# A state-space scan emitted beside local attention and feed-forward, with its input replicated over states by DMA

## The chip, the cores and the metric

The kernel runs on one core of one Trainium2 chip. The metric is device time in microseconds (us) of one execution; lower is better. The core's engines are PE (TensorE: matmuls and transposes; PEld is its weight load), DVE (VectorE), ACT (ScalarE), POOL (GpSimd) and SP (SyncE), which here only issues DMAs. Each engine works through its own queue of instructions in order and waits on semaphores for the others. Everything is in fp32.

## What is computed

The input x has 32 sequences of 256 tokens of width 256. The output is x plus a two-layer attention and feed-forward network applied to the result of a state-space block:

```python
# state-space block (d_inner 512, 16 states)
xr, gate = split(x @ W_in.T); xr = xr + t_emb
xc = silu(causal_conv4(xr) + b_conv)
xn = layernorm(xc) * ln_g + ln_b
Bm, Cm, dt = split(xn @ W_xproj.T)            # 16 columns each
dt = tanh(dt @ W_dt.T + b_dt) * 0.01
Ad = 1 + dt * (-tanh(A_log)); Bd = Bm * min(norm(xn), 1)
h  = clip(h * Ad_t + Bd_t * xn_t, -10, 10)    # 256 steps, h is 16 x 512
y_t = sum over states of C_t * h
out = ((y + D * xn) * silu(gate)) @ W_out.T
# then twice: x += local_attention(shift(x)); x += geglu(layernorm(shift(x)))
```

The attention has 8 heads of 64 and windows of 128 tokens, each of which sees itself and the window before; q and k are normalized and rotated. The feed-forward has 682 hidden columns and uses gelu.

## The kernel before, in words

**Groups and stages.** The 32 sequences are worked on in four groups of eight (`GB`). One group's scan (`group_scan`, line 195) writes the group's residual `res`, and then two layers of `attention` (L472) and `feed_forward` (L617) update it in place; we call these two the blocks. The main loop (L712 to L720) emits scan, layer 0, layer 1 for group 0, then the same for group 1, and so on. `res` has one buffer, and scan, attention and feed-forward each open tile pools of their own and close them, so that each stage may use all of SBUF and all eight PSUM banks. All layer weights are loaded once at the start.

**The scan.** First the projection, the 4-tap convolution and silu are done for the whole group (L206 to L240: PE L210, ACT L221, POOL L226, DVE L231, ACT L236). Then there are 16 blocks of 16 steps. `prep` makes for a block of 128 (step, sequence) tokens the normalized `xn` (transposed on PE, L264; statistics L270), transposes it again (L293) to project B, C and dt (L301), and brings these through narrow products (L309 to L355) into the layout in which the scan needs them: 8 sequences x 16 states on the 128 partitions, steps in the free dimension. The kernel scales the state by the running product of Ad, so that a step is a clipped addition whose limits `lim` are scaled too. For each step, PE makes `bx` in PSUM (L413), which replicates a token's xn over its sequence's 16 states and multiplies by B: the stationary operand `lb` holds a diagonal of B values, 32 rows by 128 columns. DVE then computes one step (L421), `h_new = clip(h_old + bx)`, with one custom instruction of 128x512. For every four steps, PE sums over states with the C values (L429): the stationary operand is 128 x 32, and each of the four steps fills its own 32 rows of the PSUM tile `y`. At the end of a block, `z = (xn*D + y) * silu(gate)` is made (L439 to L441), transposed (L444) and, every four blocks, projected into `res` (L458, L465). The gate is a product of each block (L376).

**The blocks.** For a sequence, attention makes v, q and k of both windows (L497), squares and sums q and k (L508, L510), takes the inverse root with a POOL power (L192), rotates (L518 to L527) and transposes (L530). Then come, four or two heads at a time, the scores (L553), mask and maximum (L561, L565), exponential with sum (L569), transposition (L578), copy (L580) and the product with v (L583); every second sequence the output projection (L607) is added to `res` (L615). Feed-forward takes two sequences at once: layer normalization with transpositions (L641 to L660), two products per chunk of 128 hidden columns (L674), gelu (L682), product (L685), and after all six chunks the second projection (L692). In layer 1 it loads x (L634), adds it on POOL (L709) and stores the result (L710).

**What sets the order.** The kernel is written in a framework that finds the dependences, places the semaphores, and orders the instructions of each engine when the program is built; what is emitted earlier goes first where several instructions could go. So the order on an engine isn't that of the text: in the trace the preparation of the next scan block stands among the steps of the current one. A tile waits until a buffer of its pool and tag is free. All DMAs of the main part are issued by SP, in one order.

Of the kernel before, what the change touches and what calls it, by code (L numbers as in the profile page):

```python
# [9 lines left out]
FP = mybir.dt.float32  # L10
# [3 lines left out]
PSUM = bass.MemoryType.PSUM  # L14

# [7 lines left out]
GB = 8  # L23
TB = P // GB
NTB = S // TB
NQ = 4
NI = TB // NQ
TAPS = 4
# [11 lines left out]
def bc(ap, axis, n):  # L40

    ap = ap.unsqueeze(axis)
    shape = list(ap.shape)
    shape[axis] = n
    return ap.broadcast_to(shape)


@with_exitstack
def kernel(
# [35 lines left out]
    xpool = ctx.enter_context(tc.tile_pool(name="xg", bufs=1))  # L85
    rpool = ctx.enter_context(tc.tile_pool(name="res", bufs=1))

    def load_x(g):
        t = xpool.tile([P, KM, GB, S], FP, tag="xg", name=f"xg_{g}")
        for k in range(KM):  # L90
            nc.sync.dma_start(out=t[:, k], in_=xT[:, k, g * GB : (g + 1) * GB, :])
        return t
# [5 lines left out]

    w_in_sb = loaded(w_inT, [P, KM, 2 * DI], "w_in_sb", nc.sync)
# [3 lines left out]
    xg = load_x(0)  # L103
# [3 lines left out]
    wx_sb = loaded(w_xT, [P, NC_, 3 * NS], "wx_sb")  # L107
    wdt_sb = loaded(w_dtT, [NS, NS], "wdt_sb")
    bdt_sb = loaded(b_dt.partition_broadcast(P), [P, NS], "bdt_sb")
    a_sb = loaded(a_log.partition_broadcast(P), [P, NS], "a_sb")  # L110
    w_out_sb = loaded(w_outT, [P, NC_, DM], "w_out_sb")
    wqkv_sb = loaded(wqkv, [P, L, KM, 3 * DI], "wqkv_sb", nc.sync)
    wo_sb = loaded(wo, [P, L, NC_, DM], "wo_sb", nc.sync)
    flg_sb = loaded(f_ln_g, [P, L, KM], "flg_sb")
    flb_sb = loaded(f_ln_b, [P, L, KM], "flb_sb")
    w1_sb = loaded(w1, [P, L, KM, 2 * HID], "w1_sb", nc.sync)
    b1_sb = loaded(b1, [P, L, 2, len(MCH)], "b1_sb")
    w2_sb = loaded(w2, [P, L, len(MCH), DM], "w2_sb", nc.sync)
    b2_sb = loaded(b2, [P, L, KM], "b2_sb")

# [3 lines left out]
    def sums(name, n, src, out=None):  # L124
        t = const.tile([P, n], FP, tag=name, name=name)
        nc.vector.tensor_reduce(t if out is None else out(t), src, AX.X, ALU.add)
        return t

    tok_seq = sums("tok_seq", GB, ident.rearrange("p (r b) -> p b r", b=GB))
    tok_step = sums(  # L130
        "tok_step", TB, ident.rearrange("p (q i b) -> p q i b", q=NQ, i=NI),
        lambda t: t.rearrange("p (i q) -> p q i", i=NI),
    )
    tok_row = sums("tok_row", 32, ident.rearrange("p (q r) -> p r q", q=NQ))
    st_seq = sums("st_seq", GB, ident.rearrange("p (b n) -> p b n", b=GB))
    st_n = sums("st_n", NS, ident.rearrange("p (b n) -> p n b", b=GB))
    zero_tb = const.tile([P, TB], FP, tag="zero_tb", name="zero_tb")
    nc.gpsimd.memset(zero_tb, 0.0)

    neg_half = const.tile([P, HEADS], FP, tag="neg_half", name="neg_half")  # L140
    nc.gpsimd.memset(neg_half, -0.5)
    half = const.tile([P, 1], FP, tag="half", name="half")
# [3 lines left out]
    a_row = const.tile([P, NS], FP, tag="a_row", name="a_row")  # L146
    nc.scalar.activation(a_row, a_sb, AF.Tanh)
    nc.vector.tensor_scalar(a_row, a_row, -1.0, 0.01, ALU.mult, ALU.mult)
# [13 lines left out]

    rc_sb = const.tile([P, L, NW, 2, DH], FP, tag="rc_sb", name="rc_sb")
    rs_sb = const.tile([P, L, NW, 2, DH], FP, tag="rs_sb", name="rs_sb")
    with tc.tile_pool(name="setup", bufs=2) as setup:
# [14 lines left out]


# [7 lines left out]
    def rsqrt(pool, src, n, name):  # L189

        r = pool.tile([P, n], FP, tag=f"{name}_r", name=f"{name}_r")
        nc.gpsimd.tensor_tensor(r, src, neg_half[:, 0:n], ALU.pow)  # L192
        return r

    def group_scan(g, xg, res):


        with ExitStack() as es:
            xcp = es.enter_context(tc.tile_pool(name=f"xc{g}", bufs=1, reuse_waits="tile"))

            xc = xcp.tile([P, NC_, NTB, NQ, NI, GB], FP, tag="xc", name=f"xc_{g}")

            with tc.tile_pool(name=f"cv{g}", bufs=2, reuse_waits="tile") as cv, tc.tile_pool(
                name=f"cvp{g}", bufs=4, space=PSUM, reuse_waits="tile"
            ) as cvp:
                for j in range(GB // 2):  # L206
                    for c in range(NC_):
                        ps = cvp.tile([P, 2, S], FP, tag="ps", name="ps")
                        for k in range(KM):
                            nc.tensor.matmul(  # L210
                                ps.rearrange("p b t -> p (b t)"),
                                w_in_sb[:, k, c * P : (c + 1) * P],
                                xg[:, k, 2 * j : 2 * j + 2, :].rearrange("p b t -> p (b t)"),
                                start=(k == 0),
                                stop=(k == KM - 1),
                            )
                        xr = cv.tile([P, 2, TAPS - 1 + S], FP, tag="xr", name="xr")
                        nc.gpsimd.memset(xr[:, :, 0 : TAPS - 1], 0.0)
                        for i in range(2):
                            b = g * GB + 2 * j + i  # L220
                            nc.scalar.activation(  # L221
                                xr[:, i, TAPS - 1 :], ps[:, i, :], AF.Identity,
                                bias=cond_sb[:, c, b : b + 1],
                            )
                        acc = cv.tile([P, 2, S], FP, tag="acc", name="acc")
                        nc.gpsimd.tensor_scalar(  # L226
                            acc, xr[:, :, 0:S], wc_sb[:, c, 0:1], bconv_sb[:, c : c + 1],
                            ALU.mult, ALU.add,
                        )
                        for k in range(1, TAPS):  # L230
                            nc.vector.scalar_tensor_tensor(  # L231
                                acc, xr[:, :, k : k + S], wc_sb[:, c, k : k + 1], acc,
                                ALU.mult, ALU.add,
                            )
                        for i in range(2):
                            nc.scalar.activation(  # L236
                                xc[:, c, :, :, :, 2 * j + i].rearrange("p n q i -> p n i q"),
                                acc[:, i].rearrange("p (n i q) -> p n i q", n=NTB, q=NQ),
                                AF.Silu,
                            )  # L240

            sp = es.enter_context(tc.tile_pool(name=f"sp{g}", bufs=2, reuse_waits="tile"))
            hp = es.enter_context(tc.tile_pool(name=f"hp{g}", bufs=8, reuse_waits="tile"))
            zp = es.enter_context(tc.tile_pool(name=f"zp{g}", bufs=1, reuse_waits="tile"))
            sm = es.enter_context(tc.tile_pool(name=f"sm{g}", bufs=2, reuse_waits="tile"))
            ps_bx = es.enter_context(
                tc.tile_pool(name=f"pbx{g}", bufs=1, space=PSUM, reuse_waits="tile")
# [152 lines left out]
            for tb in range(NTB):  # L400
                xn, lb, ct, lim, sg, p_end = nxt
                if tb + 1 < NTB:
                    nxt = prep(tb + 1, p_end)
# [425 lines left out]
```

## Time and profile before

| | us |
|---|---|
| median of 3 runs (7242.7 to 7244.15) | 7243.88 |
| the profiled execution, its own time | 7238.73 |
| its span, first to last instruction | 7236.7 |
| PE busy | 6051.1 (84%) |
| DVE busy | 2972.4 (41%) |
| POOL busy | 1775.1 (25%) |
| ACT busy | 1582.7 (22%) |
| DVE idle in front of the scan step (L421) | 759.9 |
| mean clock granted to TensorE | 0.815 of full |
| bytes moved by DMA | 40.36 MB |

Busy time is the union of the intervals in which an engine executes something; of PE it is partly modelled, since matmuls are pipelined. A row of a group shows the line, the engine, the operation, the tiles as out<-in with their shapes, the count, then the busy time in us and the mean duration in ns, and behind the second bar the engine's idle time in front of these instructions and what ended it. A window's row shows busy times of all engines in a stretch of the span. A row of a load shows its size and the time from issue to landing.

### The profile page before, as it was taken

How to read it: one execution, taken by the hardware profiler on the slowest of the kernel's cores; microseconds unless marked ns; L12 is line 12 of the kernel's file. 1: busy time of each engine (PE TensorE's matmuls, PEld its weight loads, DVE VectorE, ACT ScalarE, POOL GpSimd, SP SyncE). 2: the span in 40 equal slices, each digit the busy share in tenths (PEclk: the TensorE clock that was granted, in tenths of full speed). 3: DMA queues.
4: the chain of work that ended last, by engine and by line, in shares of the span. 5: the costliest groups of instructions: out<-in, count | busy, mean ns of one | idle time of the engine just before them, and what ended most of it. 6: DMA issues, size and time to landing. Idle time of an engine off the chain costs nothing. (4 is left out here: it accounts for less than half of the span.)

```text
span 7236.7 us, 55107 instructions
## 1 busy us (share of the span) xinstructions
PE 6051.1 (84%) x19776; PEld 2809.3 (39%) x19776; DVE 2972.4 (41%) x5670; ACT 1582.7 (22%) x4134; POOL 1775.1 (25%) x1906
## 2 busy tenths in 40 slices
PE   6988888888788888888878888888887888888888
PEld 2222553553222355355322235435532223543553
DVE  4444442442444444244244444424424444442442
ACT  2001331331200133133120013313312001321331
POOL 2222320330222232033022222213302222321320
PEclk8778878888877887888888788798887778879878
DMA  2000000000000000000000000000000000000000
GB/s 76 0 1 12 1 0 0 1 6 15 3 0 0 12 0 1 0 1 6 15 3 1 0 12 1 1 0 1 6 16 2 0 0 0 1 0 0 1 6 18
DMA packets 14017, 40.36 MB, mean 6 GB/s; under 512 B 2352, under 2 KB 3376, under 8 KB 12080
## 3 DMA queue, kind: packets, MB, share of 16 engines
q1 hardware_dynamic: 10832, 34.78, 1.3%
q8 instruction: 158, 2.59, 0.1%
q10 hardware_dynamic: 2912, 2.05, 0.1%
q14 instruction: 115, 0.94, 0.0%
HBM read 28.43 MB, written 8.39 MB: 5 GB/s over the span
## 5 line engine op out<-in xcount | busy, mean ns | idle before, releaser
L421 DVE CUSTOM_DVE_ANT_0 h<-h,bx,lim 128x512 f32<-128x512 f32 x1024 | 825.4, 806 | 759.9 <-PE bx L413 705.3
L429 PE MATMUL y<-h,ly 128*32 128x512 f32 x2048 | 857.1, 766 | 10.6 <-DVE h L421 10.6
L192 POOL TENSOR_TENSOR ss_r<-ss,neg_half 128x8 f32<-128x8 f32 x256 | 421.4, 1646 | 1780.2 <-DVE ss L514 1771.4
L497 PE MATMUL ps_qkv<-wqkv_sb,res 128*128 128x512 f32 x1536 | 735.5, 601 | 0.0
L413 PE MATMUL bx<-xn,lb 32*128 32x512 f32 x2048 | 733.2, 782 | 0.0
L553 PE MATMUL sc<-kT,qT 64*128 64x128 f32 (+1 forms) x2048 | 576.8, 424 | 27.0 <-ACT kT L535 27.0
L583 PEld LDWEIGHTS ov<-v_sb,pT 128*128 128x128 f32 x3072 | 481.9, 241 | 110.3 <-issue 41.5
L583 PE MATMUL ov<-v_sb,pT 128*128 128x64 f32 x3072 | 506.7, 327 | 8.4 <-DVE pT L580 6.6
L561 DVE TENSOR_TENSOR p_sb<-sc,mask 128x512 f32<-128x512 f32 x384 | 257.4, 682 | 584.8 <-PE sc L553 434.0
L569 ACT ACTIVATE p_sb<-p_sb,nmax 128x128 f32<-128x128 f32 (+1 forms) x1024 | 453.4, 445 | 202.0 <-DVE nmax L565 196.6
L530 PE MATMUL tr_qk<-ident,rot 128*128 128x128 f32 x1024 | 181.2, 304 | 374.2 <-POOL rot L527 367.3
L674 PE MATMUL pg<-hT,w_sb 128*128 128x512 f32 (+1 forms) x768 | 420.9, 676 | 7.3 <-ACT hT L660 4.4
L192 POOL TENSOR_TENSOR ve_r<-ve,neg_half 128x1 f32<-128x1 f32 x192 | 106.9, 557 | 1184.7 <-DVE ve L649 1028.5
L685 DVE SCALAR_TENSOR_TENSOR ag<-pa,b_sb,gl 128x512 f32<-128x512 f32 x192 | 143.9, 749 | 574.4 <-PE pa L674 574.4
L553 PEld LDWEIGHTS sc<-kT,qT 64*128 64x128 f32 x2048 | 302.3, 217 | 190.5 <-ACT kT L535 90.2
L674 PE MATMUL pa<-hT,w_sb 128*128 128x512 f32 (+1 forms) x768 | 367.7, 601 | 0.0
L578 PE MATMUL tr_p<-ident,p_sb 128*128 128x128 f32 x1536 | 358.6, 348 | 4.4 <-ACT p_sb L569 4.4
L413 PEld LDWEIGHTS bx<-xn,lb 32*128 32x128 f32 x2048 | 188.3, 218 | 442.6 <-issue 439.0
L692 PE MATMUL po_f<-ag,w_sb 128*128 128x512 f32 (+1 forms) x768 | 356.9, 609 | 0.0
L450 ACT COPY zT<-tz 128x512 f32<-128x512 f32 x64 | 37.5, 586 | 1424.5 <-PE tz L444 1424.5
L497 PEld LDWEIGHTS ps_qkv<-wqkv_sb,res 128*128 128x128 f32 x1536 | 264.9, 191 | 211.4 <-issue 211.4
L526 POOL TENSOR_TENSOR rot<-rot,swp 128x512 f32<-128x512 f32 x256 | 324.7, 1268 | 69.7 <-DVE swp L523 69.7
(322 smaller groups left out, 7145.9 us busy)
## 6 DMA issues: line engine op xcount, KB each, us to landing
xg<-in_xT_dram SPq DMA_DIRECT2D x8, 1024.0 KB, 6.5
xs<-in_xT_dram SPq DMA_DIRECT2D x16, 512.0 KB, 4.1
out_dram<-fo SPq DMA_DIRECT2D x32, 256.0 KB, 2.0
wqkv_sb<-in_wqkv_dram SPq DMA_DIRECT2D x1, 3072.0 KB, 12.2
w_sb<-in_w_dram SPq DMA_DIRECT2D x1, 2728.0 KB, 12.6
w_sb<-in_w_dram SPq DMA_DIRECT2D x1, 1536.0 KB, 16.0
w_in_sb<-in_w_inT_dram SPq DMA_DIRECT2D x1, 1024.0 KB, 5.3
wo_sb<-in_wo_dram SPq DMA_DIRECT2D x1, 1024.0 KB, 4.9
```

Source lines behind the costliest of these rows:

```text
L192: nc.gpsimd.tensor_tensor(r, src, neg_half[:, 0:n], ALU.pow)
L413: nc.tensor.matmul(bx, lb[rows, i * GB : (i + 1) * GB, :].rearrange("p b n -> p (b n)"), xn[rows, :], start=True, stop=True,)
L421: nc.vector._custom_dve(TENSOR_ADD_SAT, out=h_new, in0=h_old, in1=bx, s0=lim[:, 0, t : t + 1], s1=lim[:, 1, t : t + 1],)
L429: nc.tensor.matmul(y[32 * q : 32 * q + 32, :], lyt[:, 32 * t : 32 * t + 32], hs[q], start=(i == 0), stop=(i == NI - 1),)
L497: nc.tensor.matmul(ps, res[:, k, b, t0 : t0 + W], wqkv_sb[:, l, k, a * DI : (a + 1) * DI], start=(k == 0), stop=(k == KM - 1),)
L526: nc.gpsimd.tensor_add(rot, rot, swp)
L553: nc.tensor.matmul(sc[:, i, :], qT[rows, h0 + i, w * W : (w + 1) * W], kT[rows, h0 + i, k0 : k0 + nk], start=True, stop=True,)
L569: nc.scalar.activation(p_sb[:, i, :], p_sb[:, i, :], AF.Exp, bias=nmax[:, h : h + 1], accum_out=rsum[:, h : h + 1],)
L578: nc.tensor.transpose(tr[:, i, ks], p_sb[:, i, ks], ident)
L583: nc.tensor.matmul(ov[:, h, :], pT[:, i, kb * W : (kb + 1) * W], v_sb[:, k0 // W + kb, h * DH : (h + 1) * DH], start=(kb == 0), stop=(kb = ...
L674: nc.tensor.matmul(ps[0:n, :], w1_sb[:, l, k, half_ * HID + o : half_ * HID + o + n], hT[:, k].rearrange("p b t -> p (b t)"), start=(k == ...
L692: nc.tensor.matmul(po.rearrange("p b t -> p (b t)"), w2_sb[0:n, l, m, d * P : (d + 1) * P], ag[0:n, m, :], start=(m == 0), stop=(m == len( ...
```

## The change

The whole device part is rewritten around one idea of order, in these parts.

1. **Two streams.** `group_scan`, `attention` and `feed_forward` become generators that yield after a piece of work. The first group's scan is emitted alone. Then `side_by_side` emits the blocks of group g and, in proportion (87 scan pieces to 248 block pieces), the scan of group g+1; the last group's blocks have nothing beside them. `res` has two buffers.
2. **Replication by DMA.** `xn` is written to a DRAM scratch tile `xnd` (three buffers). For every two steps one DMA of 512 KB on SP reads the eight sequences' rows 16 times, once for each state, into `xrep` (four buffers). ACT multiplies it in place by `beta`, a value per partition and step, and the DVE step takes both inputs from SBUF. `bx` and `lb` on PE and POOL are gone. D*xn is also loaded from the scratch (`xd`, four DMAs per 16 steps) and multiplied on POOL.
3. **Chunks of 32 steps.** The convolution, which was done for the whole group first, is done for each chunk, with a carry of three tokens; the gate too. A chunk's preparation is split into pieces, one after every four steps of the chunk before. xn isn't transposed a second time: the projection of B, C and dt runs on the unnormalized `xc` (64 output rows, 256 columns), and mean and inverse deviation are applied to the result; W_dt and ln_g are multiplied into the projection at the start. The result is spread to partitions by three small DMAs (`rw`). silu is computed as x*(1+tanh(x/2)), with ACT's tanh and a DVE product, and the halves go into w_out and the normalization.
4. **Memory.** All pools stay open. The blocks share five PSUM banks, the scan has three. `sq`, `swp`, `o_sb` and `hn` share one tag of two buffers, q, k and v are tiles of one window (two or three buffers), and other tags are shared too.
5. **Weights** of a layer are loaded anew in each of the eight layer passes, into single buffers.
6. **Smaller edits in the blocks.** The scores of window 1 are products of 128 instead of 256 columns; the output projection is done for each sequence (256 columns instead of 512); in feed-forward the second projection follows each hidden chunk into two banks that are held through the loop; x is added per half.

The core of the diff, shortened ("..." marks what is left out):

```diff
+CH = 32
+XR = 2
+def side_by_side(main, other, n_main, n_other):
+    done = 0
+    for i, _ in enumerate(main):
+        want = (i + 1) * n_other // n_main
+        while done < want:
+            next(other, None)
+            done += 1
+    for _ in other:
+        pass
...
-    xpool = ctx.enter_context(tc.tile_pool(name="xg", bufs=1))
-    rpool = ctx.enter_context(tc.tile_pool(name="res", bufs=1))
+    wpool = ctx.enter_context(tc.tile_pool(name="weights", bufs=1, reuse_waits="tile"))
+    rpool = ctx.enter_context(tc.tile_pool(name="res", bufs=2, reuse_waits="tile"))
...
+    sp = ctx.enter_context(tc.tile_pool(name="sp", bufs=1, reuse_waits="tile"))
+    sm = ctx.enter_context(tc.tile_pool(name="sm", bufs=2, reuse_waits="tile"))
+    hp = ctx.enter_context(tc.tile_pool(name="hp", bufs=6, reuse_waits="tile"))
+    xp = ctx.enter_context(tc.tile_pool(name="xp", bufs=4, reuse_waits="tile"))
+    dp = ctx.enter_context(tc.tile_pool(name="dp", bufs=3, space=DRAM))
+    ps_s = ctx.enter_context(tc.tile_pool(name="pss", bufs=2, space=PSUM, reuse_waits="tile"))
+    ps_y = ctx.enter_context(tc.tile_pool(name="psy", bufs=1, space=PSUM, reuse_waits="tile"))
+    ap_ = ctx.enter_context(tc.tile_pool(name="at", bufs=2, reuse_waits="tile"))
+    aw = ctx.enter_context(tc.tile_pool(name="aw", bufs=3, reuse_waits="tile"))
+    ps_w = ctx.enter_context(tc.tile_pool(name="psw", bufs=5, space=PSUM, reuse_waits="tile"))
...
+        def prep(c):
+            yield from conv_chunk(c)
...
+                    pr[0 : 4 * NS, 0 : GB * CH], wx_sb[:, ch, :], xc[:, ch],
...
+            for i in range(3):
+                nc.sync.dma_start(
+                    out=rw[:, i],
+                    in_=raw[i * NS : (i + 1) * NS].rearrange("n (b t) -> n b t", b=GB),
+                )
+            xnd = dp.tile([GB * CH, DI], FP, tag="xnd", name="xnd")
...
                 nc.gpsimd.tensor_mul(xn, xn, lng_sb)
                 nc.gpsimd.tensor_add(xn, xn, lnb_sb)
+                nc.sync.dma_start(out=xnd[j * P : (j + 1) * P], in_=xn)
...
+        def steps(c, filler):
...
+            for hb in range(CH // TB):
...
                     for q in range(NQ):
-                        bx = ps_bx.tile([P, DI], FP, tag=f"bx{q}", name=f"bx{q}")
-                        nc.tensor.matmul(
-                            bx,
-                            lb[rows, i * GB : (i + 1) * GB, :].rearrange("p b n -> p (b n)"),
-                            xn[rows, :],
...
+                        t = hb * TB + i * NQ + q
+                        if t % XR == 0:
+                            xr = xp.tile([P, XR, DI], FP, tag="xrep", name="xrep")
+                            nc.sync.dma_start(
+                                out=xr, in_=bc(xrows[:, t : t + XR, :], 0, NS)
+                            )
+                        bx = xr[:, t % XR]
+                        nc.scalar.activation(bx, bx, AF.Copy, scale=beta[:, t : t + 1])
                         h_new = hp.tile([P, DI], FP, tag="h", name="h")
                         nc.vector._custom_dve(
-                            TENSOR_ADD_SAT, out=h_new, in0=h_old, in1=bx,
+                            TENSOR_ADD_SAT, out=h_new, in0=state["h"], in1=bx,
                             s0=lim[:, 0, t : t + 1], s1=lim[:, 1, t : t + 1],
                         )
...
+                    next(filler, None)
+                    yield
...
+        yield from prep(0)
+        for c in range(NCH):
+            yield from gate_chunk()
+            nxt = prep(c + 1) if c + 1 < NCH else iter(())
+            now = steps(c, nxt)
+            yield from now
+            for _ in nxt:
+                yield
...
+    def blocks(g, res):
+        for l in range(L):
+            wqkv_sb, wo_sb, w1_sb, w2_sb = layer_weights(l)
+            yield from attention(l, res, wqkv_sb, wo_sb)
+            yield from feed_forward(g, l, res, w1_sb, w2_sb)
+    res = new_res(0)
+    for _ in group_scan(0, res):
+        pass
+    for g in range(NG):
+        if g + 1 < NG:
+            nxt = new_res(g + 1)
+            scan = group_scan(g + 1, nxt)
+        else:
+            nxt, scan = None, iter(())
+        side_by_side(
+            blocks(g, res), scan, L * (ATTN_YIELDS + FF_YIELDS), SCAN_YIELDS
+        )
+        res = nxt
```

## The prediction, made before the result was known

> **What bounds the kernel now.** I first read the busy time by stage, in windows cut where the scan lines begin and end. Columns after the window: its length, then busy us (instructions) of PE, PEld, DVE, ACT, POOL, the granted clock, the DMA share, GB/s.
>
> ```profile
> 84.00:690.00 606.00, 530.26 (x1593) 171.78 (x1593) 277.63 (x528) 47.39 (x103) 146.38 (x207) 0.77 0.01 4
> 690.00:1825.00 1135.00, 948.44 (x3286) 517.34 (x3286) 429.73 (x839) 319.90 (x867) 278.33 (x232) 0.84 0.01 4
> 850.00:880.00 30.00, 27.76 (x94) 20.18 (x95) 8.20 (x14) 8.08 (x24) 0.00 (x0) 0.50 0.00 1
> ```
>
> The first row is a scan alone, the second the two layers (attention and feed-forward, here "the blocks") of one group, the third a piece of attention in which TensorE is nearly always busy and yet has half its clock. The cuts at 690, 1825, 2497, 3635, 4303, 5440 and 6110 us give eight stages: scans of 690 (start included), 672, 668 and 670, blocks of 1135, 1138, 1137 and 1127: the span of 7236.7. The two kinds never lie beside each other, ACT is 8% busy in a scan, and DMA is idle in both. Next the groups of instructions that are costly in the scan, and the loads with their time to landing:
>
> ```profile
> L421 DVE CUSTOM_DVE_ANT_0 h<-h,bx,lim 128x512 f32<-128x512 f32 x1024 | 825.4, 806 | 759.9 <-PE bx L413 705.3
> L429 PE MATMUL y<-h,ly 128*32 128x512 f32 x2048 | 857.1, 766 | 10.6 <-DVE h L421 10.6
> L413 PE MATMUL bx<-xn,lb 32*128 32x512 f32 x2048 | 733.2, 782 | 0.0
> ```
>
> ```profile
> xg<-in_xT_dram SPq DMA_DIRECT2D x8, 1024.0 KB, 6.5
> xs<-in_xT_dram SPq DMA_DIRECT2D x16, 512.0 KB, 4.1
> lng_sb<-in_s_ln_g_dram ACTq DMA_DIRECT2D x1, 256.0 KB, 7.2
> ```
>
> A scan is a chain in which each step h on DVE waits for the product bx on PE: 705 us of DVE's waiting. In the blocks PE sets the pace: weighting its busy time by the clock in 5 us windows gives 804 us of full-clock work in 1135, or 71%.
>
> **Part by part, for one group ("a pass").** *Removed:* bx, 8 records in 1.12 us for each 4 steps (the PE timeline), 64 x 1.12 = 72 us of PE; the second transposition (tp_xn), the narrow products pd, pc, pp2, POOL's lb and xt.
>
> *PE added or kept beside the blocks,* at full clock: y, 8 records in 1.68 us when h is there, 64 x 1.68 = 108; with gaps as now 857.1/4 = 214. Input and gate projections: 24 records of L210 took 10.57 us, 0.44 each, twice 64 records = 56. w_out (L458) 64 x 0.44 = 28. Transposes 2 x 16 x 0.63 = 20. The new 64-row projection, 32 matmuls of 256 columns, 64 records at half of 0.44 = 14; selectors 3. Sum 229 to 335; I take 260, nearer the low end, since the scheduler that orders the engines already mixes preparation into the steps in the PE timeline. In the blocks, window-1 scores become 128-column pieces: 16 records of 128 columns take 1.71 us, 8 of 256 take 1.14, so 1.14 us more per sequence and layer, 16 x 1.14 = 18. The output projection per single sequence moves the same columns: nothing, or at worst one more 0.245 us weight load per record (64 a layer and pass, 31 us). **PE per overlapped pass: 804 + 260 + 18 = 1082 us at full clock.**
>
> *DVE:* three h take 2.69 us in a row, so 256 x 0.897 = 230. Per chunk of 32 steps: conv 4 x (0.41 + 4 x 0.49, half-width versions of L518/L231) = 9.5; gate 4 x 0.49 = 2; statistics 2 x 1.2; z 2 x 0.69; eight 128x128 products at 0.29 = 2.3; some fifteen small ones 3. That is 20.6 x 8 = 165. **About 400 a pass**, with the blocks' 430 it is 830. *ACT:* scaling, 256 x 0.60 (L285) to 0.69 (L682, a pointer operand), 154 to 177, plus tanh, xn, squares and copies of about 60; with 320 it is 560. *POOL:* 278 + about 130 = 410. None reaches PE.
>
> h now reads both inputs from SBUF, which no h of before does. Its nearest rows:
>
> ```profile
> L421 DVE CUSTOM_DVE_ANT_0 h<-h,bx,lim x1024: 795/807/810, 111.4 to 6094.9; 128x512 f32<-128x512 f32 x171
> L231 DVE SCALAR_TENSOR_TENSOR acc<-xr,wc_sb,acc x192: 737/747/1146, 26.1 to 5489.2; 128x512 f32<-128x512 f32 x192
> ```
>
> (min/median/max ns.) With one PSUM input the time never varies; L231, with two SBUF inputs and POOL active, usually costs its median, but reached 0.40 us more. So 0 to 0.40 us a step, 0 to 102 us a pass on DVE; below nothing has no reason, as the work is the same. I take 0.02 (mean less median of L231 is 14 ns), 5 us. The Trainium skill (SBUF — State Buffer, Who interferes with whom) speaks against the change here: a DVE instruction with two SBUF inputs and a GpSimd one that reads SBUF exclude each other for a whole instruction. By that rule alone, estimated with POOL busy 410 of 1387 us and half of its 1.27 us operation left on average, a step would lose 0.19 us, 49 us a pass, and the forecast would be some 50 to 200 us later.
>
> *DMA:* 128 replicating loads of 512 KB a pass, on SP. The next 512 KB of an ordinary load cost 6.5 - 4.1 = 2.4 us, 307 us a pass, hidden below DVE's 400. Replicated reading shows only in lng_sb: 256 KB in 7.2 us beside other loads, at worst 14.4 per 512 KB; below, 1.7 (wqkv's 3072 KB in 12.2 us against w_in's 1024 in 5.3). I take 2.4, since in the trace's packet records the 2 KB packets of these broadcast loads last a median 84 ns and SP's ordinary ones 85. Latency, 4.1 us plus ACT 0.69, is covered by four buffers, 8 steps, 7.2 us of h. SP's other issues (xd, rw, xn's write, weights, xs, out) stand in the same order; what waits behind a blocked one are xrep loads, then h, then y. Weights now load once per layer pass, 4180 KB, some 16 us (w2's landing): wqkv and wo during feed-forward, w1 and w2 during attention, so nothing; uncovered, 7 x 16 = 112 us.
>
> *First scan,* nothing beside it: the first h was at 111 us, of which the whole-group conv was some 60; conv now goes by chunks, but weight products and a DRAM round trip come first, so 90. Then DVE's 400 at 85% busy, 470: **560**, against 690. At 100% it is 490; paced as before (600), 690.
>
> *Overlapped passes:* 1082 us of PE over the share reached. As before, 71%: 1524. A 92% share is the most that I see over tens of us (27.76 of 30, though not at full clock): 1176. Two independent streams fill each other's gaps, such as the 2.8 us before each tp_hn, but queues are in order and PSUM for the blocks falls from 8 banks to 5; I take 78%: **1387**, three times 4160.
>
> *Last pass,* no scan beside it: (804 + 18)/0.71 = 1158; fewer banks and shared buffers (sq, swp, o_sb and hn in two slots) cost something, 0 to 100; I take **1200**. Tail 10.
>
> **Sum: 560 + 4160 + 1200 + 10 = 5930 us**, against the profiled run's 7238.7 (span 7236.7), itself 0.07% under the median of 7243.9.
>
> The clock: in the third row above PE is busy 93% and stays at 0.50. The Trainium skill (TensorE: Matmul & The Clock Gate, Part 1) has the full clock granted after about 3.4 us of sustained activity. Were that so for a PE kept busy 84%, a pass would take 1082/0.84 = 1288 and the sum be 5630; the row contradicts it for this mix of narrow matmuls and transposes, so the forecast stays.
>
> **Rivals.** *A, better:* scan matmuls fill the lulls after which the clock drops, and share times clock reaches 88%: 1230 a pass, last 1160, 5420 in all. For: half-clock stretches follow lulls (840 to 850 us: PE busy 46%). Against: third row.
>
> *B, no real overlap:* priorities or in-order queues run scan and blocks in turn: 560 + 3 x (430 + 1200) + 1210 = 6660. For: in the scan, PE follows h instruction by instruction (y, six records in 2.9 us). Against: the stages need different engines most, and preparation is already mixed in. That is also the case in which the change doesn't do what it says.
>
> *C, slower than before:* the replicating loads set the pace of every pass. At the upper bound, 14.4 us, a pass takes 128 x 14.4 = 1843, four make 7370, with the last blocks 8580. It decides where 4 x 128 x T + 1210 + 90 exceeds 7239: T of 11.6 us per load, sustained, whether the reads are slow or SP issues them late behind a waiting instruction. For: lng_sb's 7.2 us; before, SP stood 3078 us in front of L634 waiting for feed-forward. Against: the packet times, four loads in flight, and 10.8 us of slack per load (1387/128).
>
> **How the numbers follow.** The forecast (5650 to 6300) gets 0.58, A (under 5650) 0.14, B (6300 to 7220) 0.16, C 0.10, no change 0.02. 0.2% is about what a measurement of this kernel can tell from none. Faster 0.58 + 0.14 + 0.16 = 0.88. The range, 5300 to 6900, leaves out C and the far ends of A and B; it takes in the low and high PE shares (3 x 1176 to 3 x 1524, other terms alike: 5300 to 6340), with the 102 us of contention per pass and the 112 of weights 6860.
>
> **What will show it.** Right: h starts all through the blocks; first blocks' matmuls near 560; three passes near 1390 with PE about 90% busy and the clock near 0.85; DVE's largest wait is no longer bx; xrep lands in under 6 us. A: clock over 0.95 in the passes. B: stretches of only h and y between stretches of none. C: DVE waits for ACT's scaling, ACT for xrep, SP long in front of one issue. Wrong altogether: blocks over 1500 in the last pass, where nothing lies beside them.

## The result and the profile after

The changed kernel takes 8499.81 us (median of 4 runs, 8496.46 to 8507.69) against 7244.01 (4 runs) before: a ratio of 1.173, interval 1.171 to 1.175. It is 17% slower where 18% faster was forecast; the profiled execution has a span of 8505.9 us. We read the stages first: windows of the profile after, cut where the first scan ends and where the last feed-forward of each group ends (columns as in the prediction's windows).

```profile
84.00:515.00 431.00, 346.06 (x1040) 116.97 (x1038) 343.12 (x652) 210.52 (x373) 144.01 (x175) 0.96 0.69 175
515.00:2560.00 2045.00, 1521.76 (x5087) 835.89 (x5088) 867.60 (x1722) 610.23 (x1390) 466.56 (x486) 0.78 0.20 55
2560.00:4540.00 1980.00, 1434.63 (x4730) 799.19 (x4729) 764.28 (x1511) 550.23 (x1279) 421.33 (x419) 0.76 0.17 46
4540.00:6530.00 1990.00, 1407.36 (x4515) 804.05 (x4513) 675.75 (x1349) 504.91 (x1196) 390.52 (x373) 0.73 0.13 36
6530.00:8500.00 1970.00, 1268.12 (x3641) 773.52 (x3640) 390.49 (x799) 355.52 (x915) 276.01 (x231) 0.65 0.02 5
```

The scan does what it was meant to do. The first one ends at 515 us, and the three others lie wholly beside blocks: the passes with a scan take at most 75 us longer than the last, which has none. But every pass takes about 1980 us where blocks alone took 1135. The last row carries the most: there PE's busy time times its clock is 1268.12 x 0.65 = 824 us of full-clock work, as expected, in 1970 us.

Attention is where the time went. Taken between two stretches of feed-forward's matmuls on PE, it lasts 407 us a layer before and 805 to about 840 after, while feed-forward's stretch, 155 us a layer before, went only to about 175. One layer of attention before, and one in the last pass after:

```profile
1249.00:1656.00 407.00, 335.82 (x1325) 201.30 (x1323) 178.06 (x341) 131.07 (x383) 127.45 (x100) 0.82 0.01 3
```

```profile
6526.00:7332.00 806.00, 486.35 (x1490) 326.59 (x1490) 158.50 (x322) 150.51 (x409) 130.07 (x102) 0.60 0.02 6
```

PE is busy for 60% of the stretch instead of 83%, at a clock of 0.60 instead of 0.82. DVE, ACT and POOL have about the same work as before. So PE waits, and what it does between the waits is slower too. The groups of the profile name the wait, first after, then before:

```profile
L593 POOL TENSOR_TENSOR rn<-ss,neg_half 128x8 f32<-128x8 f32 x256 | 421.5, 1646 | 3772.4 <-DVE ss L591 3772.2
L608 PE MATMUL tr_qk<-ident,rot 128*128 128x128 f32 x1024 | 268.6, 412 | 1262.2 <-POOL rot L605 1262.2
...
L572 PE MATMUL ps_qkv<-wqkv_sb,res 128*128 128x512 f32 x1536 | 958.1, 771 | 0.0
```

```profile
L530 PE MATMUL tr_qk<-ident,rot 128*128 128x128 f32 x1024 | 181.2, 304 | 374.2 <-POOL rot L527 367.3 <-DVE oT L601 3.5
L497 PE MATMUL ps_qkv<-wqkv_sb,res 128*128 128x512 f32 x1536 | 735.5, 601 | 0.0
```

PE stands 1262 us before the transposes of q and k (374 before), and the same projection matmul takes 771 ns on average instead of 601. POOL in turn stands 3772 us before the power (L593), its chain's first instruction: no engine is busy throughout, each waits for another. One link of the chain, in the timeline of the last pass (start, duration, engine, line, and in brackets the engine's idle time before it):

```profile
6734.76 3.10 PE L572 MATMUL ps_qkv<-wqkv_sb,res 128*128 128x512 f32 x4
...
6737.90 0.60 ACT L585 ACTIVATE sq<-ps_qkv 128x512 f32<-128x512 f32 x1 [2.31 <-PE ps_qkv L572]
6738.53 0.69 DVE L587 TENSOR_REDUCE ss<-sq 128x8 f32<-128x512 f32 x1 [8.15 <-ACT sq L585]
...
6739.97 1.65 POOL L593 TENSOR_TENSOR rn<-ss,neg_half 128x8 f32<-128x8 f32 x1 [6.17 <-DVE ss L591]
6741.59 1.26 POOL L604 TENSOR_TENSOR rot<-rot,swp 128x512 f32<-128x512 f32 x1
6742.92 1.04 POOL L605 TENSOR_TENSOR rot<-rot,rn 128x512 f32<-128x512 f32 x1
...
6744.02 1.12 PE L608 MATMUL tr_qk<-ident,rot 128*128 128x128 f32 x4 [6.16 <-POOL rot L605]
...
6744.93 4.85 PE L572 MATMUL ps_qkv<-wqkv_sb,res 128*128 128x512 f32 x8
```

Square, sum, power, rotate and scale are the same instructions as before. What is new is that PE has nothing to do during these 6.16 us: the next projections stand behind the transposes. All four chains of a sequence look like this. PE's order in one sequence of attention says the same (x the number of matmuls; the trace has two records for each of them, and one for a transposition):

```
after:  ps_qkv x4, tr_qk x4, ps_qkv x2, tr_qk x4, ps_qkv x4, tr_qk x4, ps_qkv x2, tr_qk x4, sc x4, tr_p x4, ov x4, ...
before: ps_wo x8, ps_qkv x9, tr_qk x4, ps_qkv x2, tr_qk x4, ps_qkv x1, sc x8, tr_qk x4, ps_qkv x2, tr_qk x4, ps_qkv x1, ...
```

After, each q or k is projected, awaited and transposed before the next: that is the order of the text. Before, four and a half projections go ahead of the first transposes.

**The theories.** *T:* in the change all PSUM tiles of the blocks share one tag; buffers of one tag are handed out in the order of the text, so a tile that waits for its data holds back every later tile of its tag, and PE runs the blocks serially. *B:* five banks are too few. *S:* the shared SBUF buffers (sq, swp, o_sb, hn) are too few. *C:* the scan and its loads disturb the blocks (the prediction's slower rival).

### The profile page after: what moved, and what is told of

It is laid out like the page before. It is cut to its first block, busy times and chain, and to the rows that moved or that the text cites. A ratio compares the mean times of both kernels' runs of the same rounds, so it can differ in the third digit from the quotient of the medians.

```text
span 8505.9 us, 57088 instructions
## 1 busy us (share of the span) xinstructions
PE 6012.2 (71%) x19132; PEld 3356.1 (39%) x19132; DVE 3067.7 (36%) x6119; ACT 2240.8 (26%) x5171; POOL 1719.4 (20%) x1734
## 5 line engine op out<-in xcount | busy, mean ns | idle before, releaser
L593 POOL TENSOR_TENSOR rn<-ss,neg_half 128x8 f32<-128x8 f32 x256 | 421.5, 1646 | 3772.4 <-DVE ss L591 3772.2
L494 DVE CUSTOM_DVE_ANT_0 h<-h,xrep,lim 128x512 f32<-128x512 f32 x1024 | 928.1, 906 | 107.3 <-PE y L502 24.8
L572 PE MATMUL ps_qkv<-wqkv_sb,res 128*128 128x512 f32 x1536 | 958.1, 771 | 0.0
L492 ACT ACTIVATE xrep<-xrep,beta 128x512 f32<-128x512 f32 x1024 | 682.0, 713 | 326.0 <-DMA xrep<-xnd 258.7
L608 PEld LDWEIGHTS tr_qk<-ident,rot 128*128 128x128 f32 x1024 | 172.2, 205 | 1488.9 <-POOL rot L605 1487.2
L637 PE MATMUL sc<-kT,qT 64*128 64x128 f32 x3072 | 747.9, 404 | 0.0
L587 DVE TENSOR_REDUCE ss<-sq 128x8 f32<-128x512 f32 x256 | 175.3, 685 | 1385.2 <-ACT sq L585 1385.1
L637 PEld LDWEIGHTS sc<-kT,qT 64*128 64x128 f32 x3072 | 611.9, 288 | 122.8 <-issue 109.6
L662 PEld LDWEIGHTS tr_p<-ident,p_sb 128*128 128x128 f32 x1536 | 224.9, 181 | 690.3 <-ACT p_sb L653 623.4
L691 PE MATMUL ps_wo<-oT,wo_sb 128*128 128x256 f32 x1024 | 364.3, 533 | 32.1 <-ACT oT L686 31.7
```

The source lines that it names most:

```text
L492: nc.scalar.activation(bx, bx, AF.Copy, scale=beta[:, t : t + 1])
L494: nc.vector._custom_dve(TENSOR_ADD_SAT, out=h_new, in0=state["h"], in1=bx, s0=lim[:, 0, t : t + 1], s1=lim[:, 1, t : t + 1],)
L572: nc.tensor.matmul(ps, res[:, k, b, t0 : t0 + W], wqkv_sb[:, k, a * DI : (a + 1) * DI], start=(k == 0), stop=(k == KM - 1),)
L593: nc.gpsimd.tensor_tensor(rn, ss, neg_half, ALU.pow)
L608: nc.tensor.transpose(tr[:, hp_, :], rot[:, 2 * hp_ : 2 * hp_ + 2, :].rearrange("p h d -> p (h d)"), ident,)
L637: nc.tensor.matmul(sc[:, i, kb * W : (kb + 1) * W], qTs[w][rows, h0 + i, :], kTs[kw][rows, h0 + i, :], start=True, stop=True,)
```

## The experiments

The edits are shown in short form: names, pools and tags that change, and not every line.

**The scan not beside the blocks, then all banks, then four tags (e1, e2, e3).** e1 emits the scans before the blocks. e2 also closes the scan's pools, so that the blocks' one tag has eight banks. e3 divides these eight into four tags, as before the change.

```diff
# e1
-        side_by_side(blocks(g, res), scan, ...)
+        for _ in scan: pass
+        for _ in blocks(g, res): pass
# e2: scan pools closed after each scan
-ps_w = pool("psw", bufs=5)
+ps_w = pool("psw", bufs=8)
# e3: on e2
+ps_mm, ps_tr, ps_sc, ps_ov = pools of 3, 2, 2, 1
-ps_qkv, tr_qk, sc, tr_p, ov, tr_o, ps_wo: all ps_w, tag "w"
+ps_qkv, ps_wo, pa, pg: ps_mm; tr_qk, tr_p, tr_o, tp_h, tp_hn: ps_tr; sc, po_f: ps_sc; ov: ps_ov
```

> The changed kernel, with the next group's scan emitted before the group's blocks instead of beside them; all buffers, banks, tags, transfers and block code as changed. Theory T (the blocks are slow by themselves, because all of their PSUM tiles share one tag and PE therefore runs them in program order): the blocks stay at about 1970 us a group, the scans stand in turn at about 430 each (first scan: 84 to 515 us): 84 + 4 x 430 + 4 x 1970 = about 9680 us. Rival C (the scan and its replicating loads slow what lies beside them): the blocks fall back to about 1140, 84 + 4 x 430 + 4 x 1140 = about 6360 us. Rivals B (five banks are too few) and S (shared SBUF buffers are too few) expect what T does here.

> As e1_in_turn, but the scan's pools are closed when a scan ends, so the blocks' one tag has all eight PSUM banks instead of five. T (one tag is handed out in program order, however many banks it has): no change from e1_in_turn, about 9680 us, attention about 820 us a layer. B (too few banks): attention falls back to about 385 us a layer, 84 + 4 x 430 + 4 x 1140 = about 6360 us. S: as T.

> As e2_in_turn_8banks, the same eight banks divided into four tags as in the kernel before (3 for projections, 2 for transposes, 2 for scores, 1 for attention times values); the shared SBUF buffers stay as changed. T: attention near its old 385 us a layer, perhaps 450 with the shared SBUF buffers: 84 + 4 x 430 + 4 x (1140 to 1270) = 6360 to 6880 us. S (the SBUF buffers make the order serial): still about 9680 us. B: nothing beyond e2_in_turn_8banks.

Measured: e1 9256.93, e2 9874.62, e3 7072.90 us (one run each). e1 was not quite what it was meant to be: the second scan still ran beside the first group's blocks, since nothing holds the two streams apart (hence 9257 and not 9680). C falls all the same, its 6360 being far off. In e2 the stages stand in turn, and the blocks take the 1970 us of the change, with eight banks. B falls. First e2's blocks of group 0, then e3's:

```profile
520.00:2489.00 1969.00, 1268.84 (x3640) 774.22 (x3639) 389.00 (x797) 355.19 (x916) 275.67 (x230) 0.65 0.02 5
```

```profile
520.00:1790.00 1270.00, 1063.09 (x3651) 663.73 (x3650) 430.18 (x830) 330.23 (x884) 275.30 (x230) 0.76 0.03 8
```

Same instructions, same banks, same SBUF buffers; only the tags differ, and 700 us a group are back. In e2's trace PE's order is that of the change; in e3's the projections run ahead again, though never past a sequence's output projection. Each scan alone takes 430 us here.

**The mirror (e5).** The kernel before, its four attention tags made one.

```diff
-pm, ptr, psc, pov = pools of 3, 2, 2, 1
+pm = pool of 8; all attention tiles in it, tag "mm"
```

> The mirror: the kernel before, untouched but for its attention, whose eight PSUM banks in four tags (3, 2, 2, 1) become eight banks in one tag. Theory T: its attention becomes serial and goes from about 385 to about 820 us a layer, 8 layers: 7244 + 8 x 435 = about 10720 us (10300 to 11000). Rivals B (number of banks) and S (SBUF buffers): both are untouched, so 7244 us.

Measured: 10477.37 us. Attention takes 813 us a layer by the measure that gave 407: 7244 + 8 x 406 = 10492. T holds in the kernel before as well; there B and S had nothing to say.

**The change with tags (e4, e7, e8, e12).** The scan stays beside the blocks. e4 divides the five banks into four tags; e7 takes one bank from the scan for the transposes; e8 gives sq and o_sb SBUF buffers of their own, at the price of one of four xrep buffers. e12 makes one tile kind alone independent.

```diff
# e4
-ps_w = pool("psw", bufs=5)
+ps_mm, ps_tr, ps_sc, ps_ov = pools of 2, 1, 1, 1     # tiles as in e3; po_f0 in sc, po_f1 in ov
# e7: on e4
-pss 2, pstr 1
+pss 1, pstr 2
# e8: on e7
-xp 4; sq: tag "swp"; o_sb: tag "swp"
+xp 3; sq: tag "sq" (2); o_sb: tag "o" (1)
# e12: on the change
-ps_w = pool("psw", bufs=5); tr_qk in ps_w
+ps_w = pool("psw", bufs=4); tr_qk in a pool of 1 of its own
```

> The changed kernel with the scan beside the blocks, its five block banks divided into four tags (2, 1, 1, 1); nothing else. T: the blocks get their look-ahead back in part; the last pass, with nothing beside it, 1150 to 1350 us, the three overlapped passes about 1400: 515 + 3 x 1400 + 1250 = about 5960 us (5600 to 6600). B and S: still about 8500 us. C: the last pass as T has it, but the overlapped passes well above it, by some hundreds of us each.

> As e4_beside_4tags (6309 us; 2, 1, 1, 1 banks for the blocks), with a sixth bank: transposes have two, and the scan's projections, transposes and statistics have one instead of two. If a bank matters where it lets the next chain start, attention falls from 540 to about 490 us a layer and the first scan grows by 30 to 60: about 5950 us. If the scan's one bank holds it back, the first scan alone shows it, and only the overlapped passes grow if the scan becomes the longer side: 6300 to 6500 us. B (the number of banks is nothing by itself): 6309.

> As e7_beside_6banks, with sq in two buffers of its own and o_sb in one; the room comes from the replicated input, three buffers instead of four. If the shared SBUF buffers hold attention back: 40 us a layer or more below e7, so some 300 us. If not: as e7. If three buffers no longer cover the replicating load (2.4 us each by itself), the first scan grows well beyond e7's.

> The changed kernel with one edit: the transposes of q and k (tr_qk) take one bank with a tag of its own, the other block tiles share the remaining four banks under one tag. Theory T: the projections no longer queue behind the transposes that wait 6.16 us for POOL's rot, so of the four such chains in a sequence two or three lie beside others; 6 to 10 us each over 64 sequences: 8500 - 64 x (12 to 30) = 6600 to 7700 us. The scores stay in program order, so it does not reach e4's 6309. If the order within a tag is not what costs: 8500.

Measured: e4 6308.70 us (ratio to before 0.869, interval 0.867 to 0.871), e7 6201.82 (0.856, 0.854 to 0.859), e8 6251.68 (0.865, 0.861 to 0.870), e12 6891.24 (one run). The same five banks in four tags take 2191 us off the change. The sixth bank, taken from the scan, is worth 107 us, less than expected. With four tags the number of banks does count: the same blocks with nothing beside them take 1270 us with eight banks (e3), 1345 with six (last pass of e7) and 1442 with five (last pass of e4). e8 gains nothing and loses 50. Its last pass takes 1344 us, as e7's, so the buffers for sq and o_sb bring nothing there; the loss lies in the passes with a scan, where h waits 80 us for the scaled input instead of 34, with the one xrep buffer less. e12 shows how far a single edit goes: 1609 us, 25 us for each of 64 (32 sequences, two layers). In e4 the overlapped passes take 1453, 1434 and 1475 us and the last 1442. The second layer's attention in the last pass of e4, and in its first pass, with the scan beside:

```profile
5600.00:6140.00 540.00, 426.96 (x1497) 301.82 (x1495) 199.90 (x363) 122.53 (x366) 126.17 (x99) 0.66 0.02 5
...
1254.00:1770.00 516.00, 447.59 (x1932) 271.97 (x1930) 310.04 (x602) 198.23 (x510) 175.57 (x165) 0.87 0.22 60
```

The row above is without a scan, the row below with one: there PE does 435 more matmul records in less time, at a clock of 0.87 instead of 0.66.

**What is left of attention (e6, e9, e10).** e3 has 477 us a layer against 407. e6 gives sq, o_sb and hn buffers of their own, e9 undoes the split of the scores, e10 undoes also the output projection for single sequences.

```diff
# e6: on e3
-sq, o_sb, hn: tag "swp"
+sq, o_sb, hn: tags of their own, 2 buffers each
# e9: on e3
-kTs: a kT tile for each window; sc in pieces of 128 keys
+kT: one tile for both windows; sc 256 keys at once
# e10: on e9
-ps_wo for each sequence, 256 columns
+ps_wo for every second sequence, 512 columns
```

> As e3_in_turn_4tags (7073 us, attention 477 us a layer against 385 before), with sq, o_sb and hn in SBUF buffers of their own instead of two shared with swp. If the shared buffers are what is left of the loss, attention falls towards 385: 7073 - 8 x 92 = about 6340 us. If the rest lies elsewhere (output projection for each sequence, scores in 128-key pieces, the clock), about 7070 us. Expected: a small part, 6900 to 7070.

> As e3_in_turn_4tags (7073 us, attention 477 us a layer), with one kT tile for both windows of a sequence, so that a score matmul takes 256 keys at once again where the change has two of 128. The score rows of the trace: 768.6 us busy in e3 against 576.8 before, 192 us over the kernel, 24 a layer: 7073 - 192 = about 6880 us. If the clock rises with it, 6800. If PE's score time is hidden behind the other engines, 7073.

> As e9_in_turn_scores_whole, and the output projection for two sequences at once again (512 matmuls of 512 columns for 1024 of 256). Its rows: 356.0 us busy against 298.2, 58 us over the kernel: e9 less about 60 us. If these two edits are all that is left of attention's loss against the kernel before (477 against 407 us by the same measure), 7073 - 8 x 70 = about 6510 us.

Measured: e6 7065.06, e9 7048.04, e10 6536.63 us (one run each). S falls: 8 us. The scores are worth 25 us, an eighth of what their busy time promised. The pairing is worth 511 us, nine times what its matmuls account for, and brings attention to 410 us a layer and the blocks to about 1138, near the kernel before's 1135. A saving so unlike its rows had to be something else. T offers it: ps_wo ends a sequence's chain, and in the projections' tag it stands ahead of the next sequence's projections.

**The output projection in another tag (e13, e14, e15, e16, and e11).** The same one edit in four kernels. e11 is e7 with whole scores and paired output projection, before the edit; e7 with whole scores alone, the base of e16, was not run.

```diff
# e13 on e3, e14 on e11, e16 on e7 with whole scores
-po = bank(ps_mm, "mm", "ps_wo")
+po = bank(ps_ov, "ov", "ps_wo")
# e15: on the kernel before
-po = pm.tile([P, 2, S], FP, tag="mm", name="ps_wo")
+po = pov.tile([P, 2, S], FP, tag="ov", name="ps_wo")
```

> e7_beside_6banks (6202 us: scan beside the blocks, 2, 2, 1, 1 banks for the blocks, 1 for the scan's small tiles) with the scores whole and the output projection for two sequences. PE is the engine that the passes wait for, so its saving should count in all four passes: 6202 - 250 = about 5950 us. If the scan beside takes the freed time or another engine is late next: 6100 to 6200.

> As e3_in_turn_4tags (7073 us, attention 477 us a layer), one edit: the output projection's bank is taken from the tag of attention times values instead of the projections' tag; it stays one sequence at a time, 256 columns, and the scores stay in pieces. Theory T (order within a tag): the output projection ends a sequence's chain and, in the projections' tag, holds back the next sequence's projections; out of that tag every sequence may run ahead, so attention falls to e10's 410 us a layer or below: 7073 - 8 x 67 = about 6540 us or less (6200 to 6600). Rival P (pairing helped by its fewer, longer matmuls): 7073.

> e11_beside_6banks_scores_wo (5873 us) with the same one edit (output projection in the tag of attention times values; two sequences at once). T: the four pair boundaries of a layer no longer drain PE; about 10 us each over 32 boundaries at most, less where the scan fills PE beside: 5600 to 5800 us. P: 5873.

> The kernel before with the same one edit: its output projection takes the bank of attention times values, not one of the three projection banks. T: its look-ahead, which stops at every second sequence, runs on: 32 boundaries at about 10 us: 7242 - 320 = about 6900 us (6800 to 7050). P: 7242.

> As e14_beside_wo_in_ov_tag, but the output projection one sequence at a time (256 columns), as in the change. T (the order was the cost, not the halves): within 100 us of e14. P: e14 plus some hundreds of us.

Measured: e11 5873.36 us (0.810, 0.809 to 0.812), e13 6206.27 (one run), e14 5570.43 (0.769, 0.766 to 0.771), e15 6646.09 (0.917, 0.915 to 0.918), e16 5600.71 (0.773, 0.771 to 0.775). e13 settles it: single sequences, halves and split scores as in the change, and attention is down to 371 us a layer, below the kernel before. It also leaves the three banks of the projections' tag to the projections alone; that the order and not a bank is what counts, its trace shows: in e3 PE does a sequence's output projection before any of the next sequence's projections, in e13 projections of the next sequence stand among the scores, ahead of it. Here is that layer:

```profile
1056.00:1427.00 371.00, 315.04 (x1502) 211.33 (x1500) 177.47 (x350) 130.33 (x383) 126.98 (x100) 0.88 0.04 14
```

1502 records as in e3's kind of attention, and 85% busy at a clock of 0.88. e16 against e14 says that halves or pairs hardly matter: 30 us, 0.5%. e15 gives the kernel before 8% for one line; its attention falls from 407 to 329 us a layer, nearly twice the gain expected from 10 us a boundary. e14 beats both kernels. Its passes (first scan, three with a scan beside, last):

```profile
91.00:611.00 520.00, 391.83 (x1087) 135.73 (x1086) 351.80 (x668) 219.94 (x398) 134.74 (x178) 0.89 0.57 145
611.00:1867.00 1256.00, 1140.42 (x4361) 586.68 (x4361) 772.68 (x1518) 524.18 (x1247) 409.11 (x420) 0.94 0.26 71
1867.00:3123.00 1256.00, 1140.81 (x4385) 585.97 (x4384) 781.60 (x1532) 529.76 (x1265) 419.43 (x429) 0.95 0.27 73
3123.00:4379.00 1256.00, 1139.73 (x4386) 585.06 (x4386) 781.34 (x1531) 529.79 (x1266) 420.44 (x427) 0.95 0.27 73
4379.00:5568.00 1189.00, 1026.64 (x3266) 560.97 (x3265) 464.20 (x864) 302.10 (x836) 276.76 (x232) 0.79 0.03 9
```

A scan that takes 520 us alone here (first row) costs 67 us beside a pass.

**The stretched state update (e17, e18).** The update h took 906 ns on average after the change, 806 before, 878 in e13. e17 moves three operations on two SBUF tiles from POOL to DVE, on e13; e18 does it on e14.

```diff
-nc.gpsimd.tensor_mul(xn, xn, lng_sb); nc.gpsimd.tensor_add(xn, xn, lnb_sb); nc.gpsimd.tensor_mul(xd, xd, dskip_sb)
+nc.vector.tensor_mul(xn, xn, lng_sb); nc.vector.tensor_add(xn, xn, lnb_sb); nc.vector.tensor_mul(xd, xd, dskip_sb)
```

> As e13_in_turn_wo_in_ov_tag (6206 us; scans alone, 430 us each; the state update h 878 ns mean, 809 median, against 806 before), with three products and sums of two SBUF tiles (xn by its gain, plus its offset, xd by its factor) moved from POOL to DVE. Theory L (a POOL instruction that reads two SBUF tiles beside h stretches it, since h now reads two SBUF tiles itself): in the trace of e13, h is 807 ns where no POOL instruction lies beside it and some 1300 beside xn's two; so the mean falls to 815 ns or less, 60 us over the kernel, and the moved work adds about 0.7 to 1 us each to DVE, 192 of them, some 150 us: 6206 - 60 + 150 = about 6300 us in all. Rival M (the second SBUF input itself costs time): the mean stays at about 880 ns.

> e14_beside_wo_in_ov_tag (5570 us) with e17's edit: three products and sums of two SBUF tiles a chunk from POOL to DVE. In e17 it took 37 us off four scans in turn, about 10 each. Beside the blocks only the first scan, which sets the end alone, should gain: 5570 - 10 = about 5560 us; if the 95 us less of h and of POOL's work matter to the passes too, 5480; if DVE's added work comes in the way of the blocks, 5600.

Measured: e17 6169.37 us (one run), e18 5590.49 (0.773, 0.771 to 0.776). The steps of h (min/median/max ns), after, in e13 and in e17:

```profile
L494 DVE CUSTOM_DVE_ANT_0 h<-h,xrep,lim x1024: 776/809/1906, 83.8 to 5115.1; 128x512 f32<-128x512 f32 x171
```

```profile
L485 DVE CUSTOM_DVE_ANT_0 h<-h,xrep,lim x1024: 778/809/1862, 84.2 to 5134.1; 128x512 f32<-128x512 f32 x171
```

```profile
L485 DVE CUSTOM_DVE_ANT_0 h<-h,xrep,lim x1024: 773/806/1043, 81.9 to 5100.6; 128x512 f32<-128x512 f32 x171
```

In e17 the mean is 808 ns: the inputs cost nothing, POOL beside them does. The program is 37 us faster (0.6%, one run each) and not 90 slower, so the moved work found room on DVE. In e18 the mean of h falls too, from 899 ns in e14 to 848, but the time does not (20 us above e14, 0.4%, the ranges overlap): beside the blocks this loss is hidden.

## Why the prediction was wrong

**The step that failed** is the last pass, "fewer banks and shared buffers (sq, swp, o_sb and hn in two slots) cost something, 0 to 100". It cost 770 us over the 1200 forecast, and most of the overlapped passes' excess over 1387 has the same cause (2045, 1980 and 1990; 1453, 1434 and 1475 in e4). The step counted buffers, and they are not what was lost: three more banks in the one tag (e2) and more SBUF buffers (e6) change next to nothing. It did not ask in which order one tag's buffers are given out. In e2 to e3, 700 of the 835 us (1970 less 1135) come from the one tag for tr_qk, sc, ov and the rest, and about 134 from the output projection, which at every sequence instead of every second stands ahead of the next projections in one tag (e3 to e10, with 6 from the scores). With the order out of the way the banks cost something too, and more than the 0 to 100: 172 us from eight to five (e3 against e4's last pass). Text and profile of before had what was needed: the description of the kernel says that a tile waits for a buffer of its pool and tag, the diff puts all twelve kinds of PSUM tile of the blocks on the tag "w", and the timeline of before shows the next sequence's projections among the current one's scores, which no single order of the text could give.

**The share that PE reaches.** "PE per overlapped pass: 1082 us at full clock" was right within a few per cent: e14's passes have 1140 x 0.945 = 1077, where its whole scores leave 1064 of the forecast's sum. So was the 822 of the last pass (824). The shares were not: instead of 71% the last pass of the change reaches 42% (824 of 1970). "In the blocks PE sets the pace" did not hold for the kernel before either: e15 has the same matmuls and takes 603 us less, so its 71% held a wait that another order removes. With the tags divided and nothing else changed (e4) the passes take 1453, 1434 and 1475 us against the 1387 of the 78%, and the last 1442 against 1200. With the output projection in another tag as well, a sixth bank, whole scores and paired sequences (e14) the share is 86% (1077 of 1256), above the 78% and below the 88% of rival A. e11, at 5873, is the nearest to 5930.

**First scan:** 560 forecast, 515 measured. **DVE, ACT and POOL never reach PE:** right. **Replicating loads:** 2.4 us taken; in the first scan the 128 loads and all else keep the DMA engines 69% busy for 431 us, at most 2.3 us a load. SP's waits in the profile after, in total us, times and the longest:

```profile
SPq L135 <- PE ps_qkv L572: 3102.0, 7, 728.0
SPq L488 <- DVE h L494: 1099.1, 311, 29.0
```

SP waits with the next loads for h to free a buffer. One sign of C was there: ACT's scaling waits 259 us in all for loads. But h waits only 24 us for ACT, so the loads do not set the pace. Rival C put the end on the right side for the wrong reason: its sum has 1210 us for the last pass, which took 1970 with no scan beside it. **Weights:** the first row is SP holding the next layer's weights until the current layer's last projection; PE waits for none of these loads in the profile after, nor in e10's, which reloads them too and whose blocks take about 1138 us against 1135 before. **B, no real overlap:** false; the scans lie beside the blocks.

**The state update:** 0.02 us a step taken, 0.10 measured, inside the bounds of 0 to 0.40, and the reason is the one that the bounds came from. The Trainium skill (SBUF — State Buffer, Who interferes with whom) gave 0.19 by estimate; it has the kind right, the size was half, and not every POOL instruction that reads SBUF stretched h (last section).

**Split scores:** 18 us a pass forecast, 25 us over the whole kernel measured (e9). **"Wrong altogether: blocks over 1500 in the last pass"** is the sign that came true and pointed at the place.

## What to carry to other kernels

Tiles of one tag are given out in the order of the text: when a change merges tags, ask of each merged tile what stands behind it in the text and how long its own data are late, however many buffers there are. A long wait on one engine is harmless while later work may pass it, and the cheapest test is to give the waiting tile, or the last tile of a chain, a tag of its own. When an edit saves many times what its rows account for, look for an order that it changed.

## What the runs showed of the hardware

**The clock went with the order of the work, and added to the loss.** The layer after and the layer of e13 have the same products and last 806 and 371 us; of the difference 171 us are PE's own longer busy time (486 against 315) and the rest is idle. Attention's clock is 0.60 at 60% busy (after), 0.82 at 83% (before), 0.88 at 85% (e13), and in e14's passes, with a scan beside, 0.94 to 0.95 at 91%. Busy share alone does not set it, though: e3's attention, here cut inside a layer, is 83% busy at 0.72.

```profile
1170.00:1610.00 440.00, 365.13 (x1425) 258.84 (x1425) 164.66 (x306) 130.37 (x377) 117.45 (x91) 0.72 0.02 5
```

What else sets it was not tried. The Trainium skill (TensorE: Matmul & The Clock Gate, Part 1) has the full clock follow some 3.4 us of sustained activity; no run here tried stretches of different length, so that this is what separates these kernels is not shown. Work beside other work came cheap: in e4 the passes with a scan were about as fast as the one without, at clocks of 0.87 and 0.66 in the two rows shown. That the scan's matmuls raised the clock is likely, but no run changed the clock alone.

**POOL stretches a DVE instruction that reads two SBUF tiles.** Worked out from the records after: 587 steps of h with no POOL instruction beside them average 806 ns, 204 with POOL busy beside them for at least 85% of their time 1118. Steps that touch a product or a sum of two SBUF tiles average 1392 (rot, L605) and 1283 (xn, L405); those that touch the convolution's first product, which reads one tile (L327, 34 steps), 818. Before, with one input of h in PSUM, 237 steps with POOL beside them for at least 85% average 807.
